# A graph network kernel: the seams between its passes rearranged, and early sums taken by node

## The chip, the core and the metric

The kernel runs on one core of a Trainium2 chip. The metric is the device time of one execution in microseconds (us). The engines are TensorE (PE, with its weight loads as PEld), VectorE (DVE), ScalarE (ACT), GpSimd (POOL) and SyncE (SP). Each executes its own list of instructions in order; DMA transfers are issued from SP's, ACT's and POOL's lists.

## The reference

There are 6250 nodes with 64 features and 206250 directed edges (src, dst), sorted by dst; they are 100000 undirected pairs in both directions and a loop at each node. Each of four layers adds to x what it makes of h, the rectified layer norm of x:

```python
h = relu(layernorm(x)); x = x + conv(relu(conv(h, W3, b3)), W4, b4)   # two convolutions, D^-1/2 (A+I) D^-1/2
h = relu(layernorm(x)); x = x + gathered(h)                           # D^-1/2 A D^-1/2 h
h = relu(layernorm(x)); x = x + messages(h, edge_attr)
h = relu(layernorm(x)); x = x + (h + S h + S S h + S S S h) / 4       # S = D^-1/2 A D^-1/2
```

A message of edge (s, d) is sigmoid(e Bw + Bb) * Vp[s] + (e Cw + Cb), where e is the edge's features after a network of two layers (w1, w2) and Vp is made of the nodes' features (pAw, pBw). Messages are clipped from below, squared, summed by d, divided by the number of edges, and the square root is taken.

## The kernel before

**The matrix.** Nodes are 49 blocks of 128, in 7 chunks of 7 blocks (W = 896 nodes). The adjacency matrix A, with small counts in 8-bit floats, is built in 14 strips of 448 columns and written to DRAM. A piece A[c][:, blocks(k), :] is 7 blocks by 896 columns, 784 KB. A node's value is held as three bf16 parts whose sum is exact enough (`split`, line 709, writes them into a tile U3 or V3), so one product with a piece is 49 matmuls of 192 columns.

**First layer.** While strips are built, the first convolution multiplies them as they are (`spread`, line 742: features by nodes, moving 448 columns, one of two halves of PE at a time). `hidden(c)` (line 947 on) turns a chunk's sums to nodes (`to_nodes`, line 735) and sends them through W3 and W4, in steps between which other work can stand. The last strip has no strip after it, so `hidden(6)` stands alone. `gather` (line 1001) is the second convolution: for each chunk c of results, 7 pieces k are loaded from SP's queue into a ring of buffers (`apool`, 8 of them) and each gives 49 matmuls into four accumulators `p_acc` (line 1016), that were set to zero by matmuls with `zeros` (line 1013). Four reduces (line 1024) add the three parts, and `then(c, z)` does the rest: `convolved` in gather 1, `turned` in gather 2. `turned` ends in Vp (written to `Vp_dram`, line 1082).

**Preparation of the messages** (lines 1096 to 1160): weights and biases, the src and dst numbers of the edges as tiles of 128 by 202 by 8 (loads at lines 1128 and 1130, in runs of 8 numbers), and operations on 1616 columns that make of dst the lanes within a window (lines 1139 to 1150) and check that each edge falls into it.

**Messages.** 202 groups of 1024 edges. `slot(i)` is one step of a pipeline over the groups; in it PE, ACT and DVE follow an order written out by hand (`manual_schedule`), while POOL and SP keep the order in which things are issued. Group i's features are turned (line 1287), pass two layers (1291, 1295), and give gate and shift four slots later (1301, 1305, 1310); POOL fetches the rows of Vp by 8 indirect DMAs (1279), into one of four buffers; DVE multiplies, adds and clips (1314 to 1316), ACT squares, DVE splits (1377, 1389), and a matmul with a 0/1 matrix `to` (1326) sums by node (1333), read at 1341 and added to H (1346).

Beside this a list `todo` holds items, of which each slot takes as many as bring the list to its end when the next chunk of nodes ends. `crossed` (line 1182 on) compares a block of A with its mirror image: transposes by PE (1188) and one read by DVE (1194), in all 392. When all groups of a chunk have been summed, `finished(c)` (line 1247) makes its new node values (a chain of DVE and ACT, 1250 to 1255, `normed`, `split`), and `plan` puts in the list: pieces of A for that chunk's part in gather 3 (`piece`, three buffers), crossings of some of them, and `partial(i, s)` (line 1201), which multiplies one half piece by the chunk's values with `spread` (21 matmuls of 448 columns, half of PE each) and has DVE add the result to Y (copy at 1210 for the first chunk, add at 1212), features by nodes. So the sums of chunk i for gather 3 are made during the slots of chunk i+1. Nothing is planned after the last chunk.

**The last layer.** After the slots comes `finished(6)`; then the products of chunk 6 are taken in 14 strips, added to Y (line 1461), turned to nodes (`to_nodes`) and passed to `propagated` (line 1429 on), which makes V3. Gathers 3 and 4 follow, like gather 2; the last writes out.

Of the kernel before, what the change touches and what calls it, by code (L numbers as in the profile page):

```python
# [11 lines left out]
I32 = mybir.dt.int32  # L12
# [583 lines left out]
QN = 32  # L596
DRIFT = 32
# [19 lines left out]
def fast(ctx, tc, bad, x, src, dst, edge_attr, W3, b3, W4, b4, w1, b1, w2, b2, Bw, Bb, Cw, Cb,  # L617
# [47 lines left out]

    node = ctx.enter_context(tc.tile_pool(name="node", bufs=1, reuse_waits="tile"))
# [24 lines left out]
    def normed(h, X_c):  # L691

        m = stat.tile([P, CB], F32, name="m")
        nc.vector.tensor_reduce(m, X_c, axis=AX.X, op=OP.add)
        nc.vector.tensor_scalar_mul(m, m, 1.0 / D)
        nc.vector.tensor_sub(h, X_c, over_features(m))
        q = stat.tile([P, CB, D], F32, name="q")
        nc.vector.tensor_mul(q, h, h)
        v = stat.tile([P, CB], F32, name="v")
# [3 lines left out]
        nc.vector.scalar_tensor_tensor(h, h, 0.0, over_features(v), op0=OP.max, op1=OP.mult)  # L703
# [5 lines left out]
    def split(u, U3, c):  # L709
        u3 = U3[:, blocks(c), :, :]  # L710
        nc.scalar.activation(u3[:, :, 0, :], u, AF.Copy)
        r = stat.tile([P, CB, D], F32, name="r")
# [39 lines left out]
    nc.scalar.dma_start(X, x.rearrange("(b p) f -> p b f", p=P))  # L752
    early = ExitStack()
    early_pool = early.enter_context(tc.tile_pool(name="early_pool", bufs=1, reuse_waits="tile"))
    with ExitStack() as ph:
# [55 lines left out]
        spool = ph.enter_context(tc.tile_pool(name="spool", bufs=3, reuse_waits="tile"))  # L811
# [14 lines left out]
        with ExitStack() as ps:  # L826
# [101 lines left out]
            for c in range(NC):  # L928
                u = wpool.tile([P, CB, D], F32, name="z", bufs=2)
                nc.vector.tensor_mul(u, H0[:, blocks(c), :], over_features(norm0[:, blocks(c)]))  # L930
                split(u, U3, c)
# [4 lines left out]
            def convolve(s, strip):  # L936
# [6 lines left out]
                if s % 2 == 0:  # L943
                    y[s // 2] = wpool.tile([P, W], F32, name="y")
                nc.scalar.activation(y[s // 2][:, s % 2 * CW:(s % 2 + 1) * CW], p[:, :CW], AF.Copy)

            def hidden(c):
# [22 lines left out]
                split(u, V3, c)  # L970

            beside = []
            for s in range(CS):
# [15 lines left out]
                if s and s % 2 == 0:  # L989
                    beside.append(hidden(s // 2 - 1))  # L990
            for steps in beside + [hidden(NC - 1)]:
# [3 lines left out]
    def normed_and_split(h, U3, c, scale):  # L995
        normed(h, X[:, blocks(c), :])
        u = stat.tile([P, CB, D], F32, name="u")
        nc.vector.tensor_mul(u, h, over_features(scale[:, blocks(c)]))
        split(u, U3, c)

    def gather(apool, wpool, psum, U3, then):


        zeros = wpool.tile([P, 6 * D], BF16, name="zeros", bufs=1)
        nc.vector.memset(zeros, 0.0)
        for c in range(NC):
            p = [psum.tile([P, 512], F32, name=f"p_acc{q}") for q in range(4)]
            for k in range(NC):
                t = apool.tile([P, CB, W], COUNT, name="piece")
                nc.sync.dma_start(t, A[c][:, blocks(k), :])  # L1010
                for d in range(CB):
# [3 lines left out]
                    for b in range(CB):  # L1015
# [4 lines left out]
                            start=False, stop=(k == NC - 1 and b == CB - 1 and d in (1, 3, 5, 6)))  # L1020
            z = wpool.tile([P, CB, D], F32, name="zg")
            for q in range(4):
                n = min(2, CB - 2 * q)
                nc.vector.tensor_reduce(  # L1024
# [482 lines left out]
```

## Time and profile before

| What | us |
|---|---|
| median of five runs (4140.22 to 4170.37) | 4160.19 |
| the profiled execution / its span | 4163.33 / 4161.4 |
| PE busy (76% of the span), granted clock 0.852 on average | 3176.4 |
| DVE busy (47%) | 1975.1 |
| POOL busy (40%) | 1652.0 |
| ACT busy (30%) | 1255.2 |

The stages by the timeline: tables and the first strip to 163; strips beside the first convolution to 577; `hidden(6)` to 592; gather 1 to 797; gather 2 to 1029; preparation to 1068; messages to 3690; the last chunk's products and the rest of gather 3's first chunk to 3777; the rest to the end. A line of the timeline gives the start, the duration, the engine, the line of the kernel, the operation, what it writes and reads, and in brackets the idle time of the engine ahead of it with what ended that. A matmul's line can hold many (xcount). "remote" stands where no releaser is seen. In the rows of 40 slices each digit is a tenth of busy share, or of the clock that PE was granted.

### The profile page before, as it was taken

How to read it: one execution, taken by the hardware profiler on the slowest of the kernel's cores; microseconds unless marked ns; L12 is line 12 of the kernel's file. 1: busy time of each engine (PE TensorE's matmuls, PEld its weight loads, DVE VectorE, ACT ScalarE, POOL GpSimd, SP SyncE). 2: the span in 40 equal slices, each digit the busy share in tenths (PEclk: the TensorE clock that was granted, in tenths of full speed). 3: DMA queues.
4: the chain of work that ended last, by engine and by line, in shares of the span. 5: the costliest groups of instructions: out<-in, count | busy, mean ns of one | idle time of the engine just before them, and what ended most of it. 6: DMA issues, size and time to landing. Idle time of an engine off the chain costs nothing.

```text
span 4161.4 us, 59158 instructions
## 1 busy us (share of the span) xinstructions
PE 3176.4 (76%) x24193; PEld 2174.9 (52%) x24193; DVE 1975.1 (47%) x3904; ACT 1255.2 (30%) x2031; POOL 1652.0 (40%) x1870
## 2 busy tenths in 40 slices
PE   1799999998466667676667667676766677789999
PEld 0566679998233334333334334343333334459999
DVE  6999943322344454444444454454445444461111
ACT  1577730000133333333333333333333233320000
POOL 4100000000566666656555566566566656610000
PEclk9999999999677777877778787787877777899999
DMA  3234355555522112222122222122222222235664
GB/s 100 72 83 110 83 164 196 186 180 115 89 67 68 44 56 73 58 71 62 56 58 76 59 73 66 53 74 57 79 55 67 55 69 61 58 107 188 198 203 151
DMA packets 280495, 388.75 MB, mean 93 GB/s; under 512 B 189225, under 2 KB 191331, under 8 KB 279955
## 3 DMA queue, kind: packets, MB, share of 16 engines
q1 hardware_dynamic: 222260, 323.17, 25.2%
q0 software_dynamic: 54112, 58.92, 6.1%
q8 instruction: 192, 3.15, 0.3%
q10 hardware_dynamic: 3840, 2.77, 0.3%
q14 instruction: 91, 0.75, 0.1%
HBM read 340.47 MB, written 44.24 MB: 92 GB/s over the span
## 4 chain that ended last, share of the span: by engine, by line
PE 52%; DVE 17%; another core or an unknown queue 12%; issue 10%; ACT 7%; DMA 2%; POOL 0%; DVEq 0%; SPq 0%; ACTq 0%; POOLq 0%
PE p_acc L1016 18%; PE p_sum L748 10%; PE p_bc L1305 6%; PE p L1291 5%; PE p_a L857 3%; DVE junk L1194 2%; PE p_s L1333 2%; DVE m L1315 2%; ACT h L1295 2%; DVE m L1314 2%; PE p_bc L1301 2%; PE p_e L1287 2%; DVE m L1377 1%; DVE m L1316 1%
## 5 line engine op out<-in xcount | busy, mean ns | idle before, releaser
L1279 POOL DMA_INDIRECT v<-Vp_dram,src_g x1616 | 1587.9, 983 | 1059.3 <-DVE m L1314 539.6
L1016 PE MATMUL p_acc<-U,piece 128*128 128x192 bf16 x9604 | 816.9, 247 | 3.4 <-DMA piece<-A 3.4
L1016 PEld LDWEIGHTS <-piece 128*128 128x128 fp8e4 x9604 | 799.5, 98 | 15.1 <-DMA piece<-A 3.9
L1305 PE MATMUL p_bc<-BC,h 128*128 128x256 f32 x1616 | 572.0, 484 | 19.6 <-issue 18.9
L1194 DVE SCALAR_TENSOR_TENSOR junk<-p_sum,there 128x512 bf16<-128x512 f32 (+1 forms) x392 | 241.8, 617 | 455.7 <-remote 357.0
L1305 PEld LDWEIGHTS p_bc<-BC,h 128*128 128x128 f32 x1616 | 336.4, 230 | 175.9 <-issue 139.7
L1188 PE MATMUL p_sum<-ident_b,piece 128*128 128x128 bf16 x1372 | 159.4, 240 | 350.9 <-DVE junk L1194 315.2
L748 PEld LDWEIGHTS <-U 128*64 128x64 bf16 x4116 | 238.4, 114 | 347.5 <-issue 206.1
L1314 DVE TENSOR_TENSOR m<-gate,v 128x512 f32<-128x512 f32 x202 | 139.9, 693 | 582.2 <-ACT gate L1310 396.7
L1188 PEld LDWEIGHTS <-piece 128*128 128x128 fp8e4 x1372 | 120.0, 108 | 509.9 <-issue 493.8
L748 PE MATMUL p_sum<-piece,U 128*64 128x448 fp8e4 x2058 | 281.9, 391 | 121.5 <-issue 76.2
L1136 POOL MEMSET origin<- 128x1 f32 (+1 forms) x194 | 6.5, 97 | 859.1 <-PE p_acc L1016 859.1
L1024 DVE TENSOR_REDUCE zg<-p_acc 128x128 f32<-128x384 f32 x112 | 56.8, 507 | 598.5 <-PE p_acc L1016 598.0
L861 ACT ACTIVATE strip<-p_a 128x784 fp8e4<-128x784 f32 x392 | 302.1, 820 | 119.5 <-PE p_a L857 103.6
L1378 ACT ACTIVATE m<-m 128x512 bf16<-128x512 f32 x202 | 127.3, 630 | 635.6 <-DVE m L1377 519.8
L1291 PE MATMUL p<-h,w_d 128*128 128x512 f32 x404 | 268.5, 750 | 60.7 <-ACT h L1295 52.5
L1295 ACT ACTIVATE h<-p,b_c 128x512 f32<-128x512 f32 x404 | 260.0, 684 | 153.7 <-remote 76.8
L1333 PE MATMUL p_s<-m,to 128*128 128x192 bf16 x1616 | 206.9, 279 | 109.1 <-DVE r_s L1341 57.0
L1291 PE MATMUL p<-eT,w_d 128*128 128x512 f32 x404 | 252.7, 711 | 14.3 <-ACT h L1295 10.5
L1321 ACT ACTIVATE m<-m 128x512 bf16<-128x512 f32 x202 | 127.2, 630 | 432.0 <-DVE m L1316 326.1
L1301 PE MATMUL p_bc<-BC_b,ones 3*128 3x512 bf16 x404 | 181.7, 450 | 92.1 <-DVE m L1315 85.0
L1333 PEld LDWEIGHTS <-to 128*128 128x128 bf16 x1616 | 174.8, 150 | 135.4 <-issue 131.6
(186 smaller groups left out, 3509.4 us busy)
## 6 DMA issues: line engine op xcount, KB each, us to landing
piece<-A SPq DMA_DIRECT2D x249, 784.0 KB
e<-in_edge_attr SPq DMA_DIRECT2D x202, 256.0 KB
A<-strip SPq DMA_DIRECT2D x14, 2744.0 KB
v<-Vp_dram,src_g POOLq DMA_INDIRECT x1616
there<-A SPq DMA_DIRECT2D x28, 784.0 KB
pairs<-pair SPq DMA_DIRECT2D x1, 1616.0 KB
Vp_dram<-v SPq DMA_DIRECT2D x7, 224.0 KB
out<-X SPq DMA_DIRECT2D x6, 224.0 KB
```

Of the source, the lines that this page charges most:

```text
L748: nc.tensor.matmul(p[half * D:(half + 1) * D, :w], U3[:, b, k, :], at_block, start=(i < 2), stop=(i >= 3 * n - 2))
L861: nc.scalar.activation(strips[s][:, :, col:col + 2 * SG].rearrange("p b (j l) -> p b j l", l=2), p[:, :, :2 * NB].rearrange("p j (b l) -> ...
L1016: nc.tensor.matmul(p[d // 2][:, d % 2 * 3 * D:(d % 2 + 1) * 3 * D], t[:, b, d * P:(d + 1) * P], U3[:, k * CB + b, :, :].rearrange("p t f - ...
L1188: nc.tensor.matmul(p[:, a - a0, :], held["here"][:, a, b * P:(b + 1) * P], ident_b, start=True, stop=True)
L1194: nc.vector.scalar_tensor_tensor(junk[:, :(a1 - a0) * P], p[:, :a1 - a0, :].rearrange("p a q -> p (a q)"), 15.5, there, op0=OP.min, op1=OP ...
L1279: nc.gpsimd.indirect_dma_start(out=v[:, j, :], out_offset=None, in_=Vp_dram[:, :], in_offset=bass.IndirectOffsetOnAxis(ap=src_g[:, g, j:j ...
L1291: nc.tensor.matmul(of[g][p], w, of[g].pop(x), start=True, stop=True)
L1295: nc.scalar.activation(of[g][t], of[g].pop(p), **how)
L1301: nc.tensor.matmul(p_bc[:, 4 * b:4 * b + 4].rearrange("p j o f -> p (j o f)"), ones, BC_b, start=True, stop=False)
L1305: nc.tensor.matmul(p_bc[:, 2 * q:2 * q + 2].rearrange("p j o f -> p (j o f)"), h2[:, q * P:(q + 1) * P], BC, start=False, stop=(k == 1))
L1314: nc.vector.tensor_mul(m, of[g].pop("gate"), of[g].pop("v"))
L1333: nc.tensor.matmul(p, to[:, :, j], m3[:, j].rearrange("p t f -> p (t f)"), start=(j == 0), stop=(j == J - 1))
```

## The change

1. `hidden(6)` is no longer run before gather 1; its steps, and then the preparation of the messages (`prepared`), stand between gather 1's pieces: two steps after each of the first five pieces, then one after each. The order of PE and DVE in gather 1 is that of the text. `zeros` is made once; the ring of gather 1 has 7 buffers.
2. In `prepared`, src and dst are loaded as rows of contiguous numbers, 101 groups at a time, on POOL's queue, copied to floats by DVE and turned by PE (32 transposes). The bias loads are on POOL's queue too.
3. `partial` works by nodes: one of four groups of a piece, of two blocks of columns (one in the last), 14 matmuls of 192 columns, then DVE reduces the three parts and adds them to Y. The list has four such items to a piece instead of two.
4. The last chunk is finished in two parts: blocks 42 to 45, whose partial sums are planned into the last slots, and blocks 46 to 48 (LATE = 3). The sums of the former chunk must be done by the end of the first part.
5. After the slots, only the three late blocks are left. `rest_of_first` multiplies them with the late part of each piece (21 matmuls), adds Y and makes V3 for one chunk of columns; two chunks go ahead, the others stand between the pieces of gather 3's first chunk. PE and DVE follow the order of the text in gathers 3 and 4.

```diff
...
+    zeros = const.tile([P, 6 * D], BF16, name="zeros")
+    nc.vector.memset(zeros, 0.0)
...
     def normed(h, X_c):
 
-        m = stat.tile([P, CB], F32, name="m")
+        n = X_c.shape[1]
+        m = stat.tile([P, CB], F32, name="m")[:, :n]
...
-    def split(u, U3, c):
-        u3 = U3[:, blocks(c), :, :]
+    def split(u, U3, at):
+        u3 = U3[:, at, :, :]
...
-                    y[s // 2] = wpool.tile([P, W], F32, name="y")
+                    y[s // 2] = (wpool if s < CS - 2 else early_pool).tile([P, W], F32, name="y")
...
-            def hidden(c):
+            def hidden(c, wpool, psum):
...
-                    beside.append(hidden(s // 2 - 1))
-            for steps in beside + [hidden(NC - 1)]:
+                    beside.append(hidden(s // 2 - 1, wpool, psum))
+            for steps in beside:
...
+    def summed_parts(z, p):
+        for q in range(4):
+            n = min(2, CB - 2 * q)
+            nc.vector.tensor_reduce(
+                z[:, 2 * q:2 * q + n, :],
+                p[q][:, :n * 3 * D].rearrange("p (d t f) -> p d f t", t=3, f=D),
+                axis=AX.X, op=OP.add)
...
-    def gather(apool, wpool, psum, U3, then):
-
-
-        zeros = wpool.tile([P, 6 * D], BF16, name="zeros", bufs=1)
-        nc.vector.memset(zeros, 0.0)
...
+                for _ in range(1 if c or k > 4 else steps):
+                    next(beside, None)
...
+            summed_parts(z, p)
             then(c, z)
...
+    def prepared(psum):
+
+        cpool = apart.enter_context(tc.tile_pool(name="cpool", bufs=1, side="right", reuse_waits="tile"))
+        before = ExitStack()
+        tpool = before.enter_context(tc.tile_pool(name="tpool", bufs=1, side="right", reuse_waits="tile"))
+        w1_d = diagonal(w1, "w1_d")
+        w2_d = diagonal(w2, "w2_d")
+        b1_c = column(b1, 2, "b1_c")
+        b2_c = column(b2, 2, "b2_c")
...
+        src_g = cpool.tile([P, G, J], I32, name="src_g")
+        dst_g = tpool.tile([P, G, J], I32, name="dst_g")
+        GH = G // 2
+        halves_of = [(ends[h * GH * P * J:(h + 1) * GH * P * J].rearrange(
+            "(g p j) -> g p j", p=P, j=J), t[:, h * GH:(h + 1) * GH, :])
+            for ends, t in ((src, src_g), (dst, dst_g)) for h in range(2)]
+        rows_i = []
+
+        def row(i):
+            rows_i.append(tpool.tile([GH, P, J], I32, name="rows_i", bufs=2))
+            nc.gpsimd.dma_start(rows_i[i], halves_of[i][0])
+
+        row(0)
+        row(1)
+        for _ in range(6):
+            yield
+        for i in range(4):
+            rows_f = tpool.tile([GH, J, P], F32, name="rows_f", bufs=2)
+            nc.vector.tensor_copy(rows_f, rows_i[i].rearrange("g p j -> g j p"))
+            if i < 2:
+                row(i + 2)
+            yield
+            for j0 in range(0, J, 4):
+                p = psum.tile([P, 4, GH], F32, name="p_turn", bufs=2)
+                for j in range(4):
+                    nc.tensor.transpose(p[:, j, :], rows_f[:, j0 + j, :], ident[:GH, :GH])
+                nc.vector.tensor_copy(halves_of[i][1][:, :, j0:j0 + 4],
+                                      p.rearrange("p j g -> p g j"))
+                yield
...
-        with tc.tile_pool(name="apool", bufs=8, reuse_waits="tile") as apool, \
+        values = []
...
+                if c == 0:
+                    values.append(of_nodes(node))
+                normed_and_split(h, values[0], blocks(c), norm3)
...
+            with tc.manual_schedule(engines={ET.PE, ET.DVE}):
+                gather(apool, wpool, psum, V3, convolved, (
+                    step for steps in (hidden(NC - 1, wpool, psum), prepared(psum))
+                    for step in steps), 2)
...
-    Y = part.tile([P, CS, CW], F32, name="Y")
+    Y = part.tile([P, NB, D], F32, name="Y")
...
+        cpool, w1_d, w2_d, b1_c, b2_c, BC, BC_b, ones, src_g, lane, own, count = made.pop()
...
-        def piece(i, k):
+
+
+        PARTS = [(c * CB, CB) for c in range(NC - 1)] + [(NB - CB, CB - LATE), (NB - LATE, LATE)]
+
+        def piece(lo, n, k):
             held["here"] = piece_pool.tile([P, CB, W], COUNT, name="piece")
-            nc.sync.dma_start(held["here"], A[k][:, blocks(i), :])
+            nc.sync.dma_start(held["here"][:, :n, :], A[k][:, lo:lo + n, :])
 
...
-        def partial(i, s):
+        def partial(i, k, d0, d1):
 
             p = ps_a.tile([P, 512], F32, name="p_sum", bufs=2)
-            for b in range(CB):
-                spread(p, U3, i * CB + b, held["here"][:, b, s % 2 * CW:(s % 2 + 1) * CW], CW,
-                       i * CB, CB)
+            lo, n = PARTS[i]
+            for d in range(d0, d1):
+                for b in range(n):
+                    nc.tensor.matmul(p[:, (d - d0) * 3 * D:(d - d0 + 1) * 3 * D],
+                                     held["here"][:, b, d * P:(d + 1) * P],
+                                     U3[:, lo + b, :, :].rearrange("p t f -> p (t f)"),
+                                     start=(b == 0), stop=(b == n - 1))
+            y = Y[:, k * CB + d0:k * CB + d1, :]
 
             def added():
+                parts = p[:, :(d1 - d0) * 3 * D].rearrange("p (d t f) -> p d f t", t=3, f=D)
                 if i == 0:
-                    nc.vector.tensor_copy(Y[:, s, :], p[:, :CW])
+                    nc.vector.tensor_reduce(y, parts, axis=AX.X, op=OP.add)
                 else:
-                    nc.vector.tensor_add(Y[:, s, :], Y[:, s, :], p[:, :CW])
+                    r = mpool.tile([P, 2, D], F32, name="r_y")[:, :d1 - d0, :]
+                    nc.vector.tensor_reduce(r, parts, axis=AX.X, op=OP.add)
+                    nc.vector.tensor_add(y, y, r)
 
             return added
...
-                    todo.append((partial, i, 2 * k))
-                    todo.append((partial, i, 2 * k + 1))
+                    for d in range(0, CB, 2):
+                        todo.append((partial, i, k, d, min(d + 2, CB)))
...
-        def finished(c):
+        def finished(part):
+
+            lo, n = PARTS[part]
+            at = slice(lo, lo + n)
...
-            if c < NC - 1:
-                plan(CROSS[c], True)
+            nc.vector.tensor_mul(t, t, over_features(some[:, at], n))
+            nc.vector.tensor_add(X[:, at, :], X[:, at, :], t)
+            normed_and_split(H[:, at, :], U3, at, norm3)
+            if part < NC - 1:
+                plan(CROSS[part], True)
+            elif part == NC - 1:
+                for k in range(NC):
+                    todo.append((piece, lo, n, k))
+                    for d in range(0, CB, 2):
+                        todo.append((partial, part, k, d, min(d + 2, CB)))
...
-        ends = [last[c * CB + CB - 1] for c in range(NC)]
+        ends = [last[lo + n - 1] for lo, n in PARTS]
...
+        def to_last(c, y):
+            if c == 0:
+                values.append(of_nodes(node))
+            propagated(c, y, values[0])
...
+        def rest_of_first():
+
+            for c in range(NC):
+                t = apool.tile([P, LATE, W], COUNT, name="late", bufs=NC)
+                nc.sync.dma_start(t, A[c][:, NB - LATE:, :])
+                p = [psum.tile([P, 512], F32, name=f"p_late{q}") for q in range(4)]
+                for d in range(CB):
+                    for b in range(LATE):
+                        nc.tensor.matmul(
+                            p[d // 2][:, d % 2 * 3 * D:(d % 2 + 1) * 3 * D],
+                            t[:, b, d * P:(d + 1) * P],
+                            U3[:, NB - LATE + b, :, :].rearrange("p t f -> p (t f)"),
+                            start=(b == 0), stop=(b == LATE - 1))
+                z = wpool.tile([P, CB, D], F32, name="zg")
+                summed_parts(z, p)
+                nc.vector.tensor_add(z, z, Y[:, blocks(c), :])
+                propagated(c, z, V3)
+                yield
+
+        with tc.manual_schedule(engines={ET.PE, ET.DVE}):
+            rest = rest_of_first()
+            next(rest)
+            next(rest)
+            gather(apool, wpool, psum, V3, to_last, rest)
+            gather(apool, wpool, psum, values[0], to_out)
...
-            if layer:
-                gather(apool, wpool, psum, U3, propagated)
-            else:
-                for s in range(CS):
-                    if s % 2 == 0:
-                        whole = apool.tile([P, CB, W], COUNT, name="piece")
-                        nc.sync.dma_start(whole, A[s // 2][:, blocks(NC - 1), :])
-                    t = whole[:, :, s % 2 * CW:(s % 2 + 1) * CW]
-                    p = psum.tile([P, 512], F32, name="p_sum", bufs=2)
-                    for b in range(CB):
-                        spread(p, U3, NB - CB + b, t[:, b, :], CW, NB - CB, CB)
-                    nc.vector.tensor_add(Y[:, s, :], Y[:, s, :], p[:, :CW])
-                    if s % 2:
-                        propagated(s // 2, to_nodes(
-                            psum, Y[:, s - 1:s + 1, :].rearrange("p s w -> p (s w)"), CB))
-            U3 = V3
```

## The prediction

> **What bounds the kernel now.** I read the page first: the busy rows and the clock row (40 slices of 104 us), then the chain of waits.
>
> ```profile
> PE   1799999998466667676667667676766677789999
> POOL 4100000000566666656555566566566656610000
> PEclk9999999999677777877778787787877777899999
> ...
> PE 52%; DVE 17%; another core or an unknown queue 12%; issue 10%; ACT 7%; DMA 2%; POOL 0%; DVEq 0%; SPq 0%; ACTq 0%; POOLq 0%
> ```
>
> PE is full in slices 2 to 9 (strips, then gathers 1 and 2) and at the end (gathers 3 and 4). In between lie the messages, 2612 us from 1068 to 3680, with PE at 69%, DVE at 47% and a lower clock: no engine bounds them alone. So three seams and one loop are to be priced. The timeline of PE shows the seams:
>
> ```profile
> 576.90 1.81 PE L739 MATMUL p_node<-twice,y 128*128 128x64 f32 x14
> 580.75 0.60 PE L731 MATMUL p_node<-ident,z 128*64 128x128 f32 x4 [2.04 <-DVE z L953]
> ...
> 588.62 3.25 PE L965 MATMUL p_node<-W4T,h 128*128 128x64 f32 x14 [0.67 <-ACT h L961]
> ```
> ```profile
> 800.97 2.36 PE L1016 MATMUL p_acc<-U,piece 128*128 128x192 bf16 x15 [3.41 <-DMA piece<-A]
> ```
> ```profile
> 1023.77 4.54 PE L1016 MATMUL p_acc<-U,piece 128*128 128x192 bf16 x53
> ...
> 1068.27 1.09 PE L1287 MATMUL p_e<-ident,e 128*128 128x128 f32 x4 [14.42 <-DMA e<-in_edge_attr]
> ```
>
> One: the last hidden step stands alone, with gaps. Two: gather 2 waits for its first piece. Three: 40 us pass between the last gather matmul and the first message transpose. The loop is seen on DVE at 2000 us:
>
> ```profile
> 2004.25 0.08 DVE L1194 DVE_READ_ACCUMULATOR junk<-p_sum,there 128x1 f32 x1
> 2019.61 0.69 DVE L1194 SCALAR_TENSOR_TENSOR junk<-p_sum,there 128x512 bf16<-128x512 f32 x1 [15.28 <-remote]
> ```
>
> Two slots run in 7 us each, then one stands still, until shortly after POOL's run of fetches has ended (POOL's last fetch there ended at 2016.1). The mean of 202 gates (1111.07 to 3680.51) is 12.8 us a slot, of which POOL's eight fetches take 8 x (0.95 + 0.30) = 10.0.
>
> **The change part by part.** The sum is made against the profiled execution, 4163.33 us (span 4161.4 and 1.9 around it); the median of the five runs is 4160.19.
>
> *Hidden step between pieces.* Now 576.90 to 591.67, 14.8 us, and the next 28 matmuls of gather 1 take 4.6 us where 28 x 84.5 ns (28.95 us for 343 matmuls, one c of gather 1) are 2.4: 17.0 in all. Its PE rows sum to 9.9 us at a granted clock of 0.69 (577 to 592), so 6.8 at full clock. Two steps follow each piece of 4.14 us, so about half of the 5.1 us of gaps stays: 9.3. Gain 7.7; 2 if every gap stays and the slow start too, 10 if none does.
>
> *First piece of gather 2.* With seven buffers instead of eight the next piece falls on one freed early: gain 3.4, at least 0.
>
> *Message preparation in gather 1.* Added on PE: 32 small transposes; the nearest row, four at 128x128, takes 0.44 to 0.60 us, so 8 groups cost 4.0. Added on DVE some 25 us, in chunks of 29 us of which the reduces and the convolved chain use 10 (70.5 of 205): hidden. But in the fixed order of DVE the first copy of the row indices stands behind the chain of the first chunk, which ends 12 us into the second one, while PE comes to the first transpose after two pieces, 8.3 us: a wait of 4.8 with the copy. Cost 8.8; 4 without the wait, 16 if two more groups wait likewise. The small loads move from ACT's queue to POOL's, which is idle then; if one lands late, only this stage hears it.
>
> *Seam before the messages.* What goes is the load of the indices, ACT's wait on the bias loads (DVE idle 9.62 us behind ACT's v), and 1616-wide DVE operations ahead of and after the last values. The same chain for the chunk before took 992.53 to 1007.20 from reduce to write, 14.7 us; now it takes 1025.46 to 1059.13, 33.7. That is 19.0 off the first fetch, which follows the write by 3.9. PE and DVE then start earlier too, with loaded edges: 20, between 14 (the write's own 3.9 grows) and 26 (the wait for edges goes too).
>
> *Early sums by node.* PE per piece: 49 x 84.5 ns = 4.14 us for two strips of 2.20. DVE per piece: three reduces of 0.557 and one of 0.356 (rows of L1024: 557, 356) and four adds of some 0.25 (between the rows of 64 columns, 0.21, and 384, 0.55), together 3.0, for two reads of 0.614:
>
> ```profile
> L1212 DVE TENSOR_TENSOR Y<-Y,p_sum x70: 600/614/623, 1949.5 to 3703.3; 128x448 f32<-128x448 f32 x70
> L1210 DVE COPY Y<-p_sum x14: 604/620/625, 1578.3 to 1883.4; 128x448 f32<-128x448 f32 x14
> ```
>
> That is +12.4 us for a chunk of seven pieces (+5.6 for the first, which has no adds): 55 us in five chunks, and PE -9. How much of it the loop feels is not shown by a row; it is bounded by two. Upwards: chunk one has no sums and 12.0 us a slot, later ones have 31 us of strips and 9 of DVE more and 12.9, 26 us for 40, a share of 0.65: +36 -6 = +30, and +55 if nothing is hidden. Downwards: only what falls in POOL's pause of 8.4 us out of 38 is felt (12), and slots with two strips, never under 10.1 us where one strip allows 7.0, become rarer: down to -30. I take +12, nearest to the pause.
>
> A rule speaks against the adds. The Trainium skill, page "SBUF — State Buffer", section "SBUF: two separate sides", says that a VectorE operation with two SBUF inputs and a GpSimd operation that reads SBUF lock each other out of a shared port for a whole instruction; the add that goes read PSUM, the one that comes does not. The trace speaks against a price: m at L1377, two SBUF inputs, took 0.69 at 2027.86 while fetches ran back to back, and 0.69 at 2049.06, when none ran. By the rule, up to a fetch of 0.94 us for each of 168 adds would be 158 us; by the row nothing. I take the row.
>
> *Last chunk in two parts.* The planner must spend 91 items in some 16 slots instead of 29, then 35 in 12. New work there: sums of four blocks, 196 x 84.5 ns = 16.6 us of PE (21 at clock 0.78) and 21 of DVE, +12 of DVE from the row above, and one more chain of finished, 5 us. With the share of 0.65 this is 38, with a quarter 15. I take 20; bounds 5 and 59 (all).
>
> *Tail.* Before, the chain of seven blocks runs from 3692.33 to 3703.4, 11.1 us, then 14 strips and turns to nodes, 45.4 us to 3748.2, then the rest of chunk one of gather 3, to 3777.0: 84.7 us.
>
> ```profile
> 3692.33 0.62 DVE L1250 TENSOR_TENSOR H<-H,n 128x448 f32<-128x448 f32 x1
> ...
> 3701.55 0.58 PE L748 MATMUL p_sum<-piece,U 128*64 128x448 fp8e4 x1 [7.40 <-ACT U L711]
> 3702.82 6.04 PE L748 MATMUL p_sum<-piece,U 128*64 128x448 fp8e4 x41 [0.69 <-ACT U L714]
> ```
>
> After: ten DVE operations of 0.62 on seven blocks shrink on three to about 0.3: 7 us. Then 7 x 21 matmuls = 12.4 us between seven pieces of 28.95, 41.4 on PE; each step's DVE chain (reduces 2.0, add 0.62, five operations of 0.62, and some 0.05 of gap behind each) is 6.3 against 5.9 on PE, so DVE leads: 7 x 6.3 + 5 for the first = 49. Sum 56, gain 28. If the two passes through ACT aren't overlapped (0.6 each), a step is 7.5 and the gain 20; if PE leads and the first costs nothing, 36.
>
> Sum: gains 7.7 + 3.4 + 20 + 28 = 59; costs 8.8 + 12 + 20 = 41; net -18: 4163 - 18 = **4145 us**.
>
> **The rivals.** *The loop pays in full.* Its DVE is near full in an unstalled slot (6.1 to 6.5 us of 7.0), so added reads lengthen every slot one for one: +55 in five chunks and +59 in the last, less the seams' 50: 4163 + 64 = 4227; with two thirds about 4190. For it: the fixed order of DVE, and slots of 7 us that have no air. Against it: DVE is at 47% and stands in stalls that end by POOL. It decides from about +0.25 us a slot (50 over 202), slower by over 0.5% from +0.35.
>
> *The loop gains.* Finer items even out the slots, and the last chunk hides in the pauses: loop -25, seams -50: 4088; with the loop at 0 4113. For it: the two-strip slots. Against it: 14 more items a chunk.
>
> *The work is moved and the wait moves too.* The first fetch waits for the last index turn, or the rest of the first layer is slowed by its chains: only half of the seams is earned, 4175. Against it: the 29-us chunks of gather 1 have the room, and gather 2 lies between.
>
> **How the numbers follow.** My forecast (seams earned, loop cost part of it, 4110 to 4175) 0.55; loop in full 0.20; loop gains 0.17; wait moved 0.08. The bound of 0.5% is 21 us, about what a measurement of this kernel can tell from no change. In hundredths the first lies 28 under it, 25 within, 2 above; the loop in full 2 within and 18 above; the loop that gains 17 under; the moved wait 2, 4 and 2. So faster 0.47, same 0.31, slower 0.22. The range for 8 in 10 leaves out the ends of the loop cases: 4095 to 4205; 4110 to 4175 is the forecast's own.
>
> **What would show it.** No PE gap over 2.1 us after the last strip, and gather 1 of about 205 to 209 us including the steps. One wait of PE of some 4 us in chunk two of gather 1. Gather 2 without an idle PE at its start. First fetch at about 20 us after the last gather reduce instead of 34. Gates: a mean of 13.0 in five chunks (12.9 + 12/145), under 14 in the last. First chunk of gather 3 done 56 us after the last finished chain began. I am wrong if the mean slot passes 13.25, or if a chunk with finer items falls below 12.5.

## The result and the profile after

The changed kernel takes 4159.95 us (median of 50 runs, 4130.95 to 4192.84), the kernel before, run beside it, 4147.06 (92 runs, 4105.73 to 4205.11). The ratio is 1.0037, with a 95% interval of 1.0024 to 1.005: some 15 us slower. Forecast were 4145 against 4163, so 18 us faster. The same kernels were met in two conditions: in one the message loop stands still again and again (the profiles of before and after, the kernel before at 4136 to 4166 us), in the other it does not (the kernel before at 3622 to 3623 us); the changed kernel met both on one chip. So each ratio below is to the kernel before in the same set of runs.

The page of the changed kernel: busy rows, clock and chain of waits.

```profile
PE   1799999998566666677666767667776766679999
...
POOL 4100010000666656656655665566566555520000
PEclk9999999999677767878778877777778788889999
...
PE 50%; DVE 19%; another core or an unknown queue 12%; issue 10%; ACT 7%; DMA 2%; POOL 1%; DVEq 0%; SPq 0%; ACTq 0%; POOLq 0%
```

The picture is that of before: PE full at both ends, a loop between that nothing bounds alone, DVE's share of the chain 19% instead of 17%. Where the time went is read from the ends of the stages: the last strip, the last reduce of each gather chunk, the first and last gate.

| Stage, us | before | after | change | forecast |
|---|---|---|---|---|
| start to the last strip | 577.0 | 575.5 | -1.5 | 0 |
| last strip to the end of gather 1's first chunk | 46.5 | 41.4 | -5.1 | -7.7 |
| gather 1, the other six chunks | 173.7 | 182.0 | +8.3 | +8.8 |
| gather 2 | 231.5 | 226.2 | -5.3 | -3.4 |
| last reduce to first gate | 83.0 | 64.0 | -19.0 | -20 |
| slots of the first chunk | 340.5 | 328.8 | -11.7 | 0 |
| slots of five chunks | 1886.3 | 1914.1 | +27.8 | +12 |
| slots of the last chunk | 342.6 | 382.9 | +40.3 | +20 |
| last gate to the end of gather 3's first chunk | 96.3 | 74.0 | -22.3 | -28 |

They sum to +11.5; the two spans differ by 11.7 (4161.4 and 4173.1). Not every row is known that well: in a second profile of the changed kernel (e19 below) the five chunks took 1872.2 us, 42 less than here, while its last chunk took 385.4.

First the seams, in the timeline of PE, changed kernel. The first piece is now waited for, the hidden step's matmuls stand between pieces, and one wait for the row indices is new:

```profile
579.32 1.33 PE L1028 MATMUL p_acc<-U,piece 128*128 128x192 bf16 x14 [3.59 <-DMA piece<-A]
...
583.86 1.70 PE L743 MATMUL p_node<-twice,y 128*128 128x64 f32 x14
```
```profile
629.07 0.93 PE L1086 MATMUL p_turn<-ident,rows_f 101*128 101x101 f32 x4 [3.80 <-DVE rows_f L1079]
```
```profile
1030.65 1.09 PE L1181 MATMUL p_node<-ident,h 128*128 128x128 f32 x4 [5.91 <-DVE h L707]
1032.48 2.08 PE L1186 MATMUL p_a<-hT,pAw_d 128*128 128x512 f32 x2 [0.75 <-ACT hT L1184]
1036.16 2.05 PE L1192 MATMUL p_v<-pBw_d,aT 128*128 128x128 f32 x8 [1.60 <-DVE aT L1189]
1042.40 1.09 PE L1358 MATMUL p_e<-ident,e 128*128 128x128 f32 x4 [4.20 <-DMA e<-in_edge_attr]
```

The last four lines are the whole chain between gather 2 and the messages; before, 15.60 us passed ahead of the first of them and 14.42 ahead of the last:

```profile
1043.91 1.09 PE L1065 MATMUL p_node<-ident,h 128*128 128x128 f32 x4 [15.60 <-DVE h L703]
```

Next the end, again PE's timeline:

```profile
3733.93 5.69 PE L1539 MATMUL p_late<-U,late 128*128 128x192 bf16 x42 [7.62 <-DVE U L719]
...
3753.22 1.90 PE L1539 MATMUL p_late<-U,late 128*128 128x192 bf16 x21
3755.89 4.20 PE L1028 MATMUL p_acc<-U,piece 128*128 128x192 bf16 x49 [0.77 <-DVE U L719]
3759.93 1.90 PE L1539 MATMUL p_late<-U,late 128*128 128x192 bf16 x21
```

A step is 6.7 us, PE's 1.9 and 4.04 and a wait of 0.77 for DVE, which leads as forecast. And the last chunk, where the loss is. These are rows of windows (columns: stretch and its length, then busy time and count of PE, PEld, DVE, ACT, POOL, then clock, share of DMA, GB/s). In both kernels the last chunk's 28 gates are cut after the twelfth; first the kernel before:

```profile
3338.00:3494.00 156.00, 117.13 (x567) 62.80 (x566) 77.20 (x165) 54.34 (x91) 92.32 (x94) 0.80 0.23 66
3494.00:3681.00 187.00, 135.93 (x661) 78.11 (x662) 96.61 (x222) 63.35 (x107) 105.05 (x107) 0.81 0.19 51
```

and those of the changed kernel:

```profile
3332.00:3501.00 169.00, 114.33 (x635) 72.54 (x636) 94.92 (x227) 53.58 (x91) 93.27 (x96) 0.81 0.24 71
3501.00:3715.00 214.00, 151.74 (x865) 97.91 (x865) 117.25 (x283) 66.57 (x113) 102.32 (x104) 0.82 0.21 58
```

POOL and ACT do the same work. DVE has 38 us more (94.92 + 117.25 against 77.20 + 96.61), PE 13 more, and the slots take 40 more.

### The profile page after: what moved, and what is told of

It is laid out like the page before. It is cut to its first block, busy times and chain, and to the rows that moved or that the text cites. A ratio compares the mean times of both kernels' runs of the same rounds, so it can differ in the third digit from the quotient of the medians.

```text
span 4173.1 us, 60079 instructions
## 1 busy us (share of the span) xinstructions
PE 3151.2 (76%) x24470; PEld 2262.1 (54%) x24470; DVE 2077.3 (50%) x4228; ACT 1256.3 (30%) x2037; POOL 1656.7 (40%) x1889
## 4 chain that ended last, share of the span: by engine, by line
PE 50%; DVE 19%; another core or an unknown queue 12%; issue 10%; ACT 7%; DMA 2%; POOL 1%; DVEq 0%; SPq 0%; ACTq 0%; POOLq 0%
PE p_acc L1028 17%; PE p_bc L1376 7%; PE p L1362 5%; PE p_sum L1263 4%; PE p_sum L752 4%; PE p_a L862 3%; DVE junk L1250 2%; DVE m L1385 2%; DVE m L1386 2%; ACT h L1366 2%; PE p_s L1404 2%; PE p_bc L1372 2%; PE p_e L1358 2%; DVE m L1387 1%
## 5 line engine op out<-in xcount | busy, mean ns | idle before, releaser
L1028 PEld LDWEIGHTS <-piece 128*128 128x128 fp8e4 x9604 | 798.9, 98 | 25.4 <-issue 14.1
L1263 PE MATMUL p_sum<-U,piece 128*128 128x192 bf16 x2254 | 265.1, 266 | 188.9 <-issue 123.7
L1244 PEld LDWEIGHTS <-piece 128*128 128x128 fp8e4 x1372 | 119.6, 110 | 516.1 <-issue 497.9
L1263 PEld LDWEIGHTS <-piece 128*128 128x128 fp8e4 x2254 | 211.7, 105 | 273.0 <-issue 258.0
L1362 PE MATMUL p<-h,w_d 128*128 128x512 f32 x404 | 276.9, 771 | 68.0 <-ACT h L1366 60.3
L752 PE MATMUL p_sum<-strip,U 128*64 128x448 fp8e4 x2058 | 236.7, 359 | 2.9 <-ACT U L715 1.4
L853 DVE TENSOR_TENSOR lo<-count,key 128x2048 bf16<-128x2048 bf16 x196 | 238.3, 1216 | 0.0
```

Of the source, the lines that this page charges most:

```text
L752: nc.tensor.matmul(p[half * D:(half + 1) * D, :w], U3[:, b, k, :], at_block, start=(i < 2), stop=(i >= 3 * n - 2))
L1028: nc.tensor.matmul(p[d // 2][:, d % 2 * 3 * D:(d % 2 + 1) * 3 * D], t[:, b, d * P:(d + 1) * P], U3[:, k * CB + b, :, :].rearrange("p t f - ...
L1244: nc.tensor.matmul(p[:, a - a0, :], held["here"][:, a, b * P:(b + 1) * P], ident_b, start=True, stop=True)
L1263: nc.tensor.matmul(p[:, (d - d0) * 3 * D:(d - d0 + 1) * 3 * D], held["here"][:, b, d * P:(d + 1) * P], U3[:, lo + b, :, :].rearrange("p t ...
L1362: nc.tensor.matmul(of[g][p], w, of[g].pop(x), start=True, stop=True)
```

## The experiments

Theory 1, formed on the table: the loop feels added engine time at a share of 0.5 to 0.65, wherever it stands, so that the sums by node and the second part of the last chunk cost more than the tail and the seams bring. Rivals: the squeezed list of the last chunk, or the number and order of the finer items, cost and not the engines' time.

### One set with standstills: seams, whole last chunk, a dose for DVE

Kernel before 4166.1 us. **e1_seams** takes the first half of the change alone; the loop's items, Y, `finished` and the tail are those of before.

```diff
-    Y = part.tile([P, NB, D], F32, name="Y")
+    Y = part.tile([P, CS, CW], F32, name="Y")
...
-        def piece(lo, n, k):
+        def piece(i, k):
...
-        def partial(i, k, d0, d1):
+        def partial(i, s):
...
-        def finished(part):
+        def finished(c):
...
-        def rest_of_first():
...
+                for s in range(CS):
```

> The changed first half (hidden step and message preparation between gather 1's pieces) with the message loop, the list of items and the tail of the kernel before. Both theories: the stages up to the first gate of the changed kernel, so about -22 us against the kernel before (4147 to 4125, ratio 0.9946), with the loop at 12.7 to 12.9 us a slot. If the loss lies in the first half instead, the ratio is 1.000 or above.

Measured: 0.9973 (0.9938 to 1.0007), half of what was expected, with an interval that holds the expected 0.9946 and 1.000 too. Its stages: gather 1 226.2, gather 2 226.2, last reduce to first gate 65.4, five chunks 1898.1, last chunk 345.1, tail 96.2. The two gathers and the seam are 17 us shorter than before (21 in the changed kernel's profile); the loop and the tail are as before.

**e2_whole** leaves the last chunk whole.

```diff
-LATE = 3
+LATE = 7
-        PARTS = [(c * CB, CB) for c in range(NC - 1)] + [(NB - CB, CB - LATE), (NB - LATE, LATE)]
+        PARTS = [(c * CB, CB) for c in range(NC)]
```

> The changed kernel with its last chunk left whole: all seven blocks stay behind the messages and the rest of the first pass takes 49 matmuls for each chunk of columns. Theory 1 (the loop feels added DVE and PE time at a share of 0.5 to 0.65, wherever it stands): five chunks +28, last chunk +7 instead of +40, tail -10 instead of -22, first half -22: about +2 us, ratio 1.000. Rival (the loss is the squeezed list of the last chunk, sums by node cost little): five chunks +5, ratio 0.995.

Measured: 1.000 (0.9965 to 1.0035), as theory 1 had it. Last chunk 351.6, tail 84.7, five chunks 1934.7. So the split is what makes the last chunk long (382.9), and it brings only 10.7 us in the tail.

**e3_dose** adds reads on DVE.

```diff
             def added():
+                spare = mpool.tile([P, CW], F32, name="spare", bufs=1)
+                nc.vector.tensor_copy(spare, p[:, :CW])
+                nc.vector.tensor_copy(spare[:, :192], p[:, :192])
```

> e1_seams with two extra DVE reads of each strip's sums (448 and 192 columns, 0.9 us together, into a tile that nobody reads), some 12.6 us a chunk: as much DVE time as the sums by node add, with the items, the list and PE unchanged, in six chunks. Theory 1: share 0.5 to 0.65 of 76 us, 38 to 49 us above e1_seams, ratio 1.004 to 1.006. Rival (DVE time is hidden, the finer items or their order cost): within 10 us of e1_seams, ratio 0.995 to 0.997.

Measured: 0.998 (0.9949 to 1.0011), 4163.2 us against 4158.4 of e1_seams, where theory 1 had 38 to 49 us between them (each ratio is known to some 13 us). Its five chunks take 1912.7 and its last 352.9: 14.7 and 7.8 us more than e1_seams' for a dose of 63 and 12.6. Theory 1 falls for the five chunks as far as DVE's time alone is meant. One profile cannot say more: the five chunks of one and the same kernel differ by 44 us from trace to trace (e2's 1934.7, and 1890.6 when it was run again as e18).

### Sets without standstills

**e5_no_sums** leaves the early sums out (Y is zero), **e6_unread** lets PE make them and DVE not read them (so Y is zero too), **e7_dose3** gives e3_dose's dose three times. All three are made from e1_seams.

```diff
-                    todo.append((partial, i, 2 * k))
-                    todo.append((partial, i, 2 * k + 1))
```
```diff
             def added():
-                if i == 0:
...
+                pass
```
```diff
+                for _ in range(3):
+                    nc.vector.tensor_copy(spare, p[:, :CW])
+                    nc.vector.tensor_copy(spare[:, :192], p[:, :192])
```

> e1_seams with the early sums left out of the list (the pieces are still loaded, Y is set to zero, so gather 3 misses six chunks of the first sum): PE -31 us and DVE -9 us for each of six chunks. If the loop feels 0.65 of added engine time, as its first chunk against the later ones suggested, 26 us a chunk: the loop falls from 2580 to about 2425. If most of it is hidden: to 2500 or above.

> As e5_no_sums, but PE makes the strips' products, which DVE does not read: e1_seams less 52 us of DVE time in six chunks. Splits the cost of the sums. If PE's time is what the loop feels: within 15 us of e1_seams. If DVE's reads are (theory 1): near e5_no_sums.

> e1_seams with three times the extra DVE reads of e3_dose: 2.7 us for each strip, 38 us a chunk, 228 us in all. e3_dose's loop was 12 us above e1_seams for 76 us. At that share of 0.16: +37 us. Theory 1 (0.5 to 0.65): +114 to +148 us. If DVE has room for the first dose only and is then the bound: above +100 us.

The kernel before takes 3622.2 us here; e5 0.9904 (0.9886 to 0.9922), e6 0.9987 (0.9977 to 0.9996), e7 1.0034 (1.0022 to 1.0047). The expectations were in microseconds of a loop that is not the one met: it takes 2047, 2068 and 2082 us from first to last gate, not 2580. What can be read, from one profile each: e6 has some 31 us of PE in each of six chunks more than e5, and a loop 21 us longer; e7 has 47 us more of DVE a chunk than e6 (38 of the dose, 9 of the reads), and its five chunks of some 300 us are together 7.5 us longer (1511.2 and 1503.7). Here the loop has room for both.

**e8_squeeze** keeps the split and the squeezed list, and plans no sums for blocks 42 to 45; the tail takes all seven.

```diff
-            elif part == NC - 1:
-                for k in range(NC):
-                    todo.append((piece, lo, n, k))
-                    for d in range(0, CB, 2):
-                        todo.append((partial, part, k, d, min(d + 2, CB)))
```

> The changed kernel with the last chunk still finished in two parts and the former chunk's list still squeezed ahead of the first of them, but with no sums planned for blocks 42 to 45: the tail takes all seven blocks. Last chunk of the slots: 382.9 us in the changed kernel, 351.6 in e2_whole. If the added sums cost (33 us of PE and DVE with the finer list): 350 to 358. If the squeeze costs (91 items in 16 slots): 370 or more, of which the first 16 slots show it.

Measured: 0.9917 (0.9901 to 0.9934); last chunk 289.9, tail 81.0. In the next set the last chunk takes 288.3 with the added sums (e11) and 282.9 whole (e12): in this condition no cost of the added sums shows, and the split as a whole costs some 4 us (288.3 to 291.4 in e8, e9, e11 and e15; 282.9 to 288.8 in the six profiles of e5, e6, e10 and e12 to e14, which leave the chunk whole). What either costs in the other condition is not answered by this run.

**e9_even**, **e10_mixed**, **e11_after** (the changed kernel itself) and **e12_pairs** met the same condition (kernel before 3623.2). The edits are of e9 (on the changed kernel), e10 (on e1_seams; the last lines turn Y, by features, to nodes behind the messages) and e12 (on e2_whole).

```diff
+            if ends[NC - 2] < i:
+                more = 5 * NC if i <= ends[NC - 1] else 0
+                n = -(-(len(todo) + more) // max(ends[NC] + 1 - i, 1))
```
```diff
+        for _ in range(2 * (steps - 1)):
+            next(beside, None)
...
-        for _ in range(6):
+        for _ in range(8):
...
+            for c in range(NC):
...
+                nc.scalar.activation(Yn[:, blocks(c), :], p[:, :CB, :], AF.Copy)
```
```diff
-                    for d in range(0, CB, 2):
-                        todo.append((partial, i, k, d, min(d + 2, CB)))
+                    for d in range(0, CB, 4):
+                        todo.append((two_groups, i, k, d))
```

> The changed kernel with an even pace in the last chunk: each slot takes its share of the 91 items and of the 35 still to come, 4.3 a slot over 29 slots, instead of 5.5 in the first 16 and 2.8 in the last 12. Same work, same tail. If the squeeze costs: 15 to 30 us below the changed kernel run beside it. If the added work costs, or neither does on this chip: within 6 us of it.

> A candidate: e1_seams (sums by features, as before), with two hidden steps ahead of the first piece and the first index turn two pieces later, and with a tail that turns Y to nodes behind the last chain and takes all seven blocks by node between gather 3's pieces. Gather 1 8 us below e1_seams (223 to 226 there), tail 85 to 90 instead of 96 to 106: 16 to 25 us below e1_seams, ratio about 0.990 to 0.992.

> The changed kernel itself, beside the others. Where the loop stands still as in the profile of the kernel before (12.8 us a slot): 1.0037 as measured. Where POOL never rests (10.2 us a slot, as in e5_no_sums to e8_squeeze): loop costs vanish and the seams and the tail stay, 30 to 45 us, ratio 0.988 to 0.992.

> e2_whole with two groups of columns to one item of the list, so 77 items a chunk as in the kernel before, with the same PE and DVE work by node. If the number and order of items cost: the loop as e1_seams, 20 to 30 us below e2_whole. If the DVE time costs: as e2_whole.

Measured: e9 0.991 and e11 0.991 (both 0.9897 to 0.9923), e10 0.9973 (0.9963 to 0.9983), e12 0.9949 (0.9936 to 0.9962). So **the same changed kernel gains 33 us** where the loop does not stand still: its stages there are five chunks 1501.7, last chunk 288.3, tail 74.3. The last chunk of a kernel that leaves it whole (e12) takes 282.9: the split costs 5 us instead of 31, and brings 15 in the tail (89.2 to 74.3). The even pace changes nothing here. e12's five chunks (1505.7) are no shorter than the others', so the number of items doesn't show as a cost in this condition; it was not tried in the other. e10's miss is in its tail, 109.2 instead of 85 to 90: in PE's timeline the turns wait, and most of them run after the chain they were meant to lie beside.

```profile
3142.31 3.31 PE L1540 MATMUL p_late<-twice,Y 128*128 128x64 f32 x28 [0.41 <-DVE of_all L1470]
3151.76 15.20 PE L1540 MATMUL p_late<-twice,Y 128*128 128x64 f32 x70 [6.14 <-DVE Y L1268]
```

The 6.14 us end with the last addition to Y, which stands behind the chain in DVE's order. Its gather 1 was 223.0, where the other kernels without standstills that have the change's seams show 223.5 to 226.5; its first chunk was 40.0 against 41.6 to 44.3, so the hidden steps put ahead bring 2 to 4 us.

**e13_two** and **e14_eight** (the same edit with bufs=8) ask whether a standstill hangs on how far POOL may run ahead, **e15_even_again** repeats e9_even.

```diff
-            v = of[g]["v"] = mpool.tile([P, J, D], F32, name="v", bufs=4)
+            v = of[g]["v"] = mpool.tile([P, J, D], F32, name="v", bufs=2)
```

> The kernel before with two buffers for v instead of four, so that POOL can run ahead by two groups at most. If a standstill lasts until POOL's run of fetches ends, runs of at most two groups (20 us) shorten each standstill: on a chip with standstills the loop falls under 12.8 us a slot; on one without, v's data come later than they are needed and the loop grows above 10.2.

> The same with eight buffers. If standstills last until POOL's run ends, runs of up to seven groups make them longer but rarer: POOL idles less, and the loop nears POOL's 10.0 us a slot, from 12.8 to about 11.5 on a chip with standstills. On one without: no change, within 5 us.

> e9_even once more. On a chip with standstills, if the squeezed list of the last chunk is what made 20 of its 40 us: ratio 0.998 to 1.000 against 1.0037 of the changed kernel. If the added work did: 1.003 to 1.005. On a chip without standstills: 0.991 again.

Measured: 1.000 (0.9991 to 1.001), 0.9999 (0.9989 to 1.0009) and 0.9912 (0.9896 to 0.9929), without standstills again, so the question of the buffers is open. With two buffers the loop did not grow, although the expectation said that it would (2058.1 us, and 2057.7 with eight). The two serve as the kernel before's stages in this condition: gather 1 220.5, gather 2 231.5, last reduce to first gate 53.5, five chunks 1495, last chunk 285, tail 104.

### A last set, with standstills, of four versions side by side

The kernel before takes 4135.8 us. **e16_best** is e9_even with e10's two edits of gather 1; the others are those of the names.

> The changed kernel with the even pace of e9_even, two hidden steps ahead of gather 1's first piece and the index turns two pieces later. Gather 1 3 us shorter (223 after the last strip, as in e10_mixed). On a chip without standstills: 3 us below the changed kernel, ratio 0.990. On one with standstills: 1.000 if the squeeze costs there, 1.003 if not.

> e1_seams beside the others of this call. Without standstills: gather 1 +5, gather 2 -5, seam -18, loop and tail as before: -18, ratio 0.995. With standstills: -11 as in e1_seams.

> e2_whole beside the others. Without standstills: the loop 8 us more than e17, the tail 89 instead of 104: ratio 0.993 to 0.995. With standstills: 1.000, so 5 to 25 above e17 by the sums by node.

> The changed kernel beside the others. Without standstills: 0.991, 12 to 15 us below e18 (tail 74 instead of 89, last chunk unchanged). With standstills: 1.0037, 15 us above e18 (last chunk 383 instead of 352, tail 74 instead of 85).

| | ratio (95%) | last chunk | tail |
|---|---|---|---|
| e17, seams alone | 0.9928 (0.9899 to 0.9958) | 345.1 (e1) | 96.2 (e1) |
| e18, and sums by node, last chunk whole | 0.9967 (0.9924 to 1.001) | 349.7 | 84.3 |
| e19, the changed kernel | 1.005 (1.0018 to 1.0082) | 385.4 | 73.1 |
| e16, even pace, gather 1 edited | 1.0006 (0.9972 to 1.004) | 392.2 | 74.7 |

The two figures in e17's row are of e1's profile, because e17's profiled execution took 4165.87 us, 53 more than its median; its own are 354.6 and 96.9. The seams alone are faster (in e1, the same kernel, the interval just reaches 1), the changed kernel is slower, and the step between e18 and e19, the split, is 0.0083 or some 34 us: 36 in the last chunk, less 11 in the tail, by the profiles 25.

Where in the last chunk the 36 us lie can be read in windows, from the 178th gate to the 195th and from there to the last; e18, then e19:

```profile
3382.90:3592.70 209.80, 149.91 (x728) 94.23 (x728) 109.62 (x262) 69.86 (x119) 130.28 (x133) 0.77 0.24 60
3592.70:3667.90 75.20, 57.30 (x307) 36.04 (x305) 43.73 (x101) 25.86 (x44) 35.80 (x36) 0.84 0.14 31
```
```profile
3368.20:3610.20 242.00, 165.67 (x973) 105.96 (x973) 134.57 (x335) 73.74 (x127) 129.82 (x133) 0.81 0.23 61
3610.20:3686.30 76.10, 57.45 (x301) 36.19 (x300) 43.95 (x103) 25.52 (x44) 35.01 (x36) 0.84 0.24 64
```

The first part's chain of e19 starts at 3594.1, and the first addition to Y of the sums of blocks 42 to 45 at 3609.35, at the end of the first window. So 32 of the 36 us are lost by the time these sums begin, in the slots with the squeezed list of the former chunk, where DVE has 25 us more to do; the slots that hold the added sums are as long as the same slots of e18 (76.10 and 75.20), which hold the end of its list. The changed kernel's first profile has 246.4 and 77.1. The even pace of e16 thins the first stretch only in part (22 additions to Y instead of 30) and does not shorten it (253.8, last chunk 392.2); its ratio is lower than e19's, with intervals that overlap, and 5 us of that are gather 1's (220.5 against 226.1). So the split costs, and it costs where the list is squeezed; that a less squeezed list would cost less is not shown, for the slots that are freed by it are needed for the added sums, and no run with standstills has the one without the other.

### The two conditions in one kernel

e11_after and e19_after_again are one kernel on one chip, at 3590 and 4165 us. ACT's timeline behind the seam, e11_after:

```profile
1051.71 0.69 ACT L1366 ACTIVATE h<-p,b_c 128x512 f32<-128x512 f32 x1 [0.39 <-PE p L1362]
1052.43 0.60 ACT L1366 ACTIVATE eT<-p_e 128x512 f32<-128x512 f32 x1
1053.23 0.69 ACT L1366 ACTIVATE h<-p,b_c 128x512 f32<-128x512 f32 x1 [0.20 <-PE p L1362]
```

and e19_after_again:

```profile
1070.47 0.69 ACT L1366 ACTIVATE h<-p,b_c 128x512 f32<-128x512 f32 x1 [7.02 <-remote]
1088.72 0.60 ACT L1366 ACTIVATE eT<-p_e 128x512 f32<-128x512 f32 x1 [17.57 <-remote]
```

The waits that end without a visible releaser are there in one and not in the other (between 1500 and 2500 us e11_after has none on any engine; the longest on DVE in e19_after_again is 16.2 us). POOL's group between 1500 and 2500 us, e11_after:

```profile
L1350 POOL DMA_INDIRECT v<-Vp_dram,src_g x776 | 764.8, 986 | 236.5 <-issue 220.0 <-DMA v<-Vp_dram,src_g 13.4 <-DVE Y L1276 1.5
```

and e19_after_again:

```profile
L1350 POOL DMA_INDIRECT v<-Vp_dram,src_g x615 | 603.2, 981 | 397.4 <-DVE m L1385 217.3 <-issue 171.2 <-DMA v<-Vp_dram,src_g 8.2
```

A fetch takes the same 0.98 us. Without standstills POOL makes 776 in 1000 us and waits 1.5 us for an engine: it is the bound, 10.3 us a slot, and work on DVE and PE beside it is nearly free (e6, e7). With them it makes 615 and waits 217 us for DVE's m.

## Why the prediction was wrong

**Where it held.** The message seam (-20, measured -19.0, and 63.3 to 65.4 us instead of 83.0 in all kernels with standstills that have it), the preparation in gather 1 (8.8 and 8.3, with the one wait of 3.80 us forecast as 4.8 with its copy), gather 2 (3.4 and 5.3), and that DVE leads the tail (6.3 us a step forecast, 6.7 measured). The five chunks were forecast at +12 within -30 and +55; the profile shows +27.8, and five profiles with sums by node lie between 1872 and 1935 against 1886, 1898 and 1905 of the three with strips: the runs don't tell this term better than to some 25 us. Of the signs, the first fetch came 16.9 us after the last reduce (forecast 20), one PE gap, the 3.59 us ahead of the first piece, was over the 2.1 that were named, and the mean slot was 13.06 us and that of the five chunks 13.20, so neither of the two signs of being wrong appeared.

**The step that failed** is "*Last chunk in two parts* ... I take 20; bounds 5 and 59". Measured are 40.3 in the table; the two other profiles that split the chunk (385.4 and 392.2) lie 40 to 50 above the 342.6 and 345.1 of a whole chunk with strips, and all three 31 to 43 above the 351.6 and 349.7 of a whole chunk with sums by node. The working had 38 by the share of 0.65 that chunk one against the later chunks gave, and 15 by a quarter; it took the lower half. This alone turns -18 into +2. That 38 comes near does not confirm its terms: they are the added sums, the additions and the second chain, while 32 of the 36 us in e19 lie ahead of the added sums, in the slots with the squeezed list. The step names that squeeze (91 items in 16 slots) and gives it no term. Nor could its sign, under 14 us a slot in the last chunk, catch the miss: 12.24 before and +20 make 12.95, and the measured 13.67 is under 14 too.

**Smaller misses.** The tail brought 23, counted from the start of the last chain (3727.39 to 3788.9, 61.5 us, where 84.7 were before), not 28: the chain took 6.5 where 7 was priced, but the steps were 6.7 instead of 6.3, and PE waited for DVE 2.67 us ahead of the first piece and 2.50 ahead of the last. The hidden step brought 5.1 and not 7.7, because the first piece lands only 3.59 us after PE is ready for it: a transfer that the hidden step had covered, and which the prediction did not price (with hidden steps put ahead of the piece, in e10 and e16, the wait fell to 2.06 and 1.95 and this stage took 40.0 and 39.9). Together +7. The slots of the first chunk are 12 us shorter, which nothing here explains; in the profiles with standstills they take 326 to 341 us.

**What was left out.** All prices of the loop were taken as if its standstills belonged to the kernel. They belong to a condition that one kernel can be met in or not. Without them the forecast's direction is right (0.991, -33 us), between its own -18 and the -50 of "the loop gains" with the loop at 0. The loop did not gain there either (2067.6 us against the 2058 of e13 and e14); the tail (30 us) and the seams do. With them the loop's cost outweighs the seams. The range, 4095 to 4205, held the median of 4159.95; the sign was wrong.

**Of the rivals**, "the loop pays in full" (+114) is too dear and "the loop gains" is excluded where standstills are. The moved wait did not come: gather 2 and the seam are shorter by 24 us, and the first fetch comes earlier than forecast. The rule of the Trainium skill weighed in the prediction, page "SBUF — State Buffer", section "SBUF: two separate sides" (a VectorE operation with two SBUF inputs and a GpSimd operation that reads SBUF shut each other out for a whole instruction), did not show in the additions:

```profile
L1276 DVE TENSOR_TENSOR Y<-Y,r_y x168: 224/292/366, 1916.7 to 3734.2; 128x128 f32<-128x128 f32 x126, 128x64 f32<-128x64 f32 x42
```

No addition took over 0.37 us, while POOL's fetches were busy for 1552 of the 2626 us of the slots, and the view of this line lists no idle time of DVE ahead of the additions.

**Open.** What makes the standstills, and whether their length hangs on POOL's runs; what the sums by node cost in five chunks where standstills are (e18 against e17: 0.0039, where each ratio is known to 0.003 or 0.004); and whether the split could be had without the squeezed list's loss. Y in three parts (e4), one addition in place of a reduce and an addition, did not fit into memory and gave no result.

**Which version.** With standstills the seams alone are fastest (0.9928 in e17, 0.9973 in e1); without them the changed kernel and e9 (0.991). No version was the best in both.

## What to carry to other kernels

When work is moved into a loop, ask also what is pushed together to make room for it, and give that a price of its own: here 11 us of tail were bought for 36 us of slots, most of them ahead of the moved work. A share read from the same trace (one chunk with and one without such work) gave 38 for the last chunk, but 49 for a dose of DVE reads that cost some 5 (e3): it is a bound, not a price. Before half of it is taken in the hope that pauses hide the rest, a run should show that they do. When a seam is closed, ask which transfer the closed gap had covered. And when idle time has no visible releaser, find out first whether the same kernel always has it: a loop at the pace of another engine and a loop with standstills put opposite signs on one change.

## What was unexpected of the hardware

The same kernel on the same chip took 3590 us in one set and 4165 in another, with equal durations of a fetch (0.98 us) and, in the slower, waits of 7 to 18 us on ACT and DVE without a visible releaser while POOL issued its fetches. The granted clock of PE in the slots from 1100 to 2500 us was 0.84 and 0.77 in the two.
